# Neighbours' rows of places 640 to 960: a one-hot matmul gather replaced by indirect DMAs from lists made on the chip

## The chip, the cores and the metric

The kernel runs on one core of a Trainium2 chip. The metric is device time in microseconds (us). The core has a matrix engine (PE), three engines for elementwise work (DVE for vectors, ACT for activations and copies, POOL for everything irregular) and a queue engine (SP). Each takes its instructions in order; they wait for one another by semaphores. DMAs are issued from the queues of SP, ACT and POOL.

## The reference

Sixteen graphs of 1024 nodes with 64 channels. Layer 0 aggregates neighbours by quantiles, layer 1 is a three-step graph convolution. Both are preceded by a layer norm with relu and added to their input. Cut to what matters here:

```python
h = jnp.maximum(_layernorm(x, axis=-1), 0.0)
# layer 0: drop some neighbours of nodes with more than 10, keep each node itself
rem = neigh & (sk > 1) & (rank % sk == sk - 1) & mask[:, :, None]
rem = rem | jnp.swapaxes(rem, 1, 2)
nd = jnp.where(rem, 0.0, adj_) > 0
s = jnp.sort(jnp.where(nd[..., None], h[:, None, :, :], jnp.inf), axis=2)
nv = nd.sum(2)
for tau, w in ((0.25, 0.25), (0.5, 0.5), (0.75, 0.25)):
    pos = tau * (nv - 1)               # linear interpolation between the two nearest ranks
    agg += w * (v_lo + frac * (v_hi - v_lo))
x = x + (relu((h + agg) @ W1 + b1) @ W2 + b2) * mask
# layer 1: h = relu(layernorm(x)); three times relu(adj @ (h @ W) + b) with a batch norm
x = x + relu(concat(x1, x2, x3) @ Wl + bl)
```

So every node needs, channel by channel, the values of its 9 to 42 live neighbours in sorted order around three ranks. That sort is most of the work.

## The kernel before, in words

**Pairs and places.** Graphs are taken two at a time (a pair, eight in all): partitions 0 to 63 hold the channels of the first graph, 64 to 127 those of the second. `prepare` (L589) and `prepare_one` (L666) load the adjacency, work out which edges stay, count the live neighbours and give each node a place by that count (L786). The rows of the live matrix are scattered to their places in DRAM by eight indirect DMAs for each graph on POOL (L793, `live_d`) and loaded again in order (L807, `lp`). `find_live` (L819) turns them on PE (L827), sums chunks, and `number_slots` (L855) numbers each node's neighbours 1, 2, 3 and on: `st.r` holds, for every possible neighbour and node, the number of the slot or something else.

**Blocks.** Places are cut into seven blocks (L39) and a tail (L44), each with a number of slots as large as its largest count: 200 nodes with 11 slots, 192 with 13, 200 with 15, 176 with 17, 120 with 19, 72 with 21, 48 with 26, and 16 with 42.

**Gather.** `gather` (L976) fills g[channel, slot, node] by a matmul with a one-hot operand. For a group of slots DVE compares the numbers with the slot (L1004, tile `s`, two buffers), PE multiplies the features, split into three bfloat16 parts `st.hp`, with it (L1035), and ACT copies the sum from PSUM (L1040).

```python
nc.vector.tensor_scalar(
    s[:, k, :, us, w0:], r[:, :, us, at + w0 : at + W], float(LIVE + 1 + k0 + k), None, ALU.is_equal
)
```

**Sort.** `quantiles` (L942) runs a fixed network of min and max on DVE (L952) over g and a spare tile t. Missing neighbours are half zeros and half large numbers (`missing_high`), so the wanted ranks lie around the middle. ACT makes the interpolation weights (L885, L888), DVE multiplies them with the few rows that can be met (L958) and sums (L967). The result has channels on partitions; `store` (L1055) turns it on PE and ACT sends it to `agg_d`.

**Order.** The order is written by hand. `weave` (L1133) runs the sort of one block and, at given shares of it, steps of other generators: the gather of the next block, and `SHARES` (L31) steps of preparing the next pair. An iteration of the loop over pairs (L1468) sorts blocks 0 to 5 and then the 48 columns (`sort_pairs`, tile `agg_pairs`) beside the next pair's first gather. The 16-column tails of four pairs are sorted together in the fifth pair and in the last. A scheduler then puts each engine's instructions in the order in which it expects them to be ready. The last pair's sorts (L1501 on, called the late stage here) run beside `later` (L1255), the second part: for each pair `first` (L1261) fetches the aggregates back by node with 16 indirect DMAs on POOL (L1274, 128 rows of 256 bytes each), adds h (L1169) and does the first layer; `second` and `next_layer` (L1192) do the convolutions (L1227, L1232, L1250). It advances 7 steps (`STEPS`) with each sort, 56 in all; the other 72 of its 128 steps follow alone (called the tail of the run here).

## Time and profile before

Three runs took 3077.79, 3082.75 and 3086.61 us. The profiled execution's own time is its span, 3081.7 us; nothing outside the span is recorded for it.

| | us | share of the span | instructions |
|---|---|---|---|
| PE, matmuls | 2579.4 | 84% | 27857 |
| DVE | 2529.1 | 82% | 5606 |
| ACT | 1702.7 | 55% | 3284 |
| POOL | 473.6 | 15% | 425 |
| mean granted PE clock | 0.925 | | |

Busy time is the union of an engine's instructions. A group of instructions is given by line, engine, operation and tiles, with its count, busy time, mean duration in ns, and the idle time of the engine just before it with what ended that. An instruction on DVE starts some 78 ns before the one ahead of it ends, so durations add up to more than busy time. The time of a DMA instruction on POOL is that of the instruction alone; when its transfer lands is recorded apart (2.5 us after its issue for L1274 and 2.6 for L793, medians).

### The profile page before, as it was taken

Reading aid. Unit: us, or ns where it says so; the run is one execution under the profiler, and the core shown is the slowest. Engines: PE = TensorE matmul, PEld = TensorE weight load, DVE = VectorE, ACT = ScalarE, POOL = GpSimd, SP = SyncE. Lnnn points to the kernel's source line nnn. Section 1 sums busy time; section 2 is a strip of 40 time slices with the busy share of each in tenths; the row PEclk is TensorE's granted clock in tenths of the full one; section 3 lists DMA queues with packets and bytes.
Section 4 is the critical chain, followed back from the end, with each engine's and each line's share of the span. In section 5 each row is a group of like instructions: output and inputs, shape, how many; then the busy total and the mean of one; then the engine's idle time right before and its main releaser. Section 6 shows DMA issues by size and latency. Waiting matters only on the chain. (4 is left out here: it accounts for less than half of the span.)

```text
span 3081.7 us, 66749 instructions
## 1 busy us (share of the span) xinstructions
PE 2579.4 (84%) x27857; PEld 1706.2 (55%) x27857; DVE 2529.1 (82%) x5606; ACT 1702.7 (55%) x3284; POOL 473.6 (15%) x425
## 2 busy tenths in 40 slices
PE   2679998989898899885888989898886789887788
PEld 1446655665566556643665566566543456554456
DVE  4049999999999999999999999999986878963332
ACT  4774676568557756774478557756753222332222
POOL 5110130031003100500031004100503120121210
PEclk9789999999999899997998999899986889999989
DMA  4131022112111211232112211211222010122211
GB/s 142 42 116 57 17 66 69 64 45 71 62 64 45 80 60 44 65 81 22 56 66 61 72 50 56 80 51 44 72 34 58 12 50 11 50 57 55 58 53 43
DMA packets 219799, 177.43 MB, mean 58 GB/s; under 512 B 187744, under 2 KB 187872, under 8 KB 215392
## 3 DMA queue, kind: packets, MB, share of 16 engines
q1 hardware_dynamic: 141824, 125.88, 13.4%
q0 software_dynamic: 15872, 37.80, 4.0%
q10 hardware_dynamic: 61792, 9.39, 2.0%
q8 instruction: 220, 3.60, 0.5%
q14 instruction: 91, 0.75, 0.1%
HBM read 124.44 MB, written 48.55 MB: 56 GB/s over the span
## 5 line engine op out<-in xcount | busy, mean ns | idle before, releaser
L1035 PE MATMUL pg<-s,hp 128*64 128x400 bf16 (+11 forms) x16848 | 1385.7, 315 | 150.5 <-DVE s L1004 132.4
L1035 PEld LDWEIGHTS <-hp 128*64 128x64 bf16 x16848 | 903.9, 113 | 532.2 <-issue 116.0
L1004 DVE TENSOR_SCALAR s<-r 128x3200 bf16<-128x3200 bf16 (+25 forms) x1312 | 624.8, 524 | 53.9 <-PE pg L1035 51.8
L793 POOL DMA_INDIRECT live_d<-edge,place x128 | 271.9, 2124 | 1831.3 <-DVE place L786 1744.0
L1040 ACT COPY g<-pg 128x400 f32<-128x400 f32 (+6 forms) x350 | 153.2, 442 | 380.4 <-PE pg L1035 368.1
L1227 PE MATMUL pg<-adjT,xw 128*64 128x512 fp8e4 x2304 | 281.9, 398 | 56.4 <-DVE xw L1217 30.6
L952 DVE TENSOR_TENSOR t<-g 128x800 f32<-128x800 f32 (+20 forms) x416 | 295.5, 733 | 2.9 <-ACT g L1040 1.9
L952 DVE TENSOR_TENSOR g<-t 128x800 f32<-128x800 f32 (+5 forms) x392 | 264.7, 703 | 0.9
L1227 PEld LDWEIGHTS <-xw 128*64 128x64 bf16 x2304 | 147.6, 115 | 174.4 <-DVE xw L1217 32.3
L1274 POOL DMA_INDIRECT agg<-agg_d,place x128 | 133.8, 1045 | 588.7 <-PE pt L1158 128.2
L683 ACT ACTIVATE edge<-a 128x1024 fp8e4<-128x1024 f32 x128 | 134.7, 1055 | 144.8 <-DMA a<-in_adj 144.6
L885 ACT ACTIVATE coef<-z,bias 128x200 f32<-128x200 bf16 (+4 forms) x392 | 150.2, 423 | 100.7 <-DVE agg L967 65.9
L888 ACT ACTIVATE coef<-coef,wcol 128x200 f32<-128x200 f32 (+6 forms) x496 | 183.6, 405 | 6.2 <-issue 3.9
L685 DVE SCALAR_TENSOR_TENSOR junk_v<-a 128x1024 fp8e4<-128x1024 f32 x128 | 155.5, 1215 | 23.2 <-DMA a<-in_adj 23.2
L952 DVE TENSOR_TENSOR t<-t 128x600 f32<-128x600 f32 (+18 forms) x272 | 169.7, 632 | 0.4
L783 ACT ACTIVATE stays<-keys,minus 128x1024 fp8e4<-128x1024 f32 x128 | 143.2, 1119 | 38.1 <-PE keys L775 35.9
L764 ACT ACTIVATE edge<-q,bias 128x1024 fp8e4<-128x1024 f32 x128 | 141.8, 1108 | 31.3 <-PE q L759 31.3
L737 ACT ACTIVATE stays<-cs,back 128x1024 f16<-128x1024 f32 x128 | 136.1, 1112 | 34.0 <-DVE look L718 18.1
L868 ACT CAST r<-pr 128x592 bf16<-128x592 f32 (+1 forms) x256 | 141.2, 585 | 19.1 <-PE pr L864 11.8
L1231 ACT ACTIVATE xT<-pg,c_L_gnn_b 128x512 f32<-128x512 f32 x48 | 32.9, 685 | 208.7 <-PE pg L1227 208.6
L830 ACT ACTIVATE liveT<-pt 128x1024 fp8e4<-128x1024 f32 x128 | 126.5, 1028 | 26.4 <-PE pt L827 21.5
L690 PE MATMUL ptE<-ident_h,edge 128*128 128x128 bf16 x1024 | 85.7, 233 | 61.7 <-ACT edge L683 45.4
(186 smaller groups left out, 3889.0 us busy)
## 6 DMA issues: line engine op xcount, KB each, us to landing
a<-in_adj SPq DMA_DIRECT2D x128, 512.0 KB, 3.5
adjT_d<-edgeT SPq DMA_DIRECT2D x16, 1024.0 KB
lp<-live_d POOLq DMA_DIRECT2D x32, 512.0 KB, 5.3
adjT<-adjT_d SPq DMA_DIRECT2D x16, 1024.0 KB, 7.0
room<-in_x SPq DMA_DIRECT2D x16, 256.0 KB, 3.6
h_d<-room SPq DMA_DIRECT2D x16, 256.0 KB
h_again<-h_d SPq DMA_DIRECT2D x16, 256.0 KB, 4.6
old_hp<-h_d SPq DMA_DIRECT2D x16, 256.0 KB, 3.6
```

The lines of the kernel that those rows point to most:

```text
L685: nc.vector.scalar_tensor_tensor(junk, a, 1.0, a, ALU.is_equal, ALU.not_equal, accum_out=odd[:, b, t : t + 1], saturate=False)
L764: nc.scalar.activation(edge[:, t, :], q, AF.Relu, bias=bias(-2.0), accum_out=nv[:, t : t + 1], saturate=False)
L783: nc.scalar.activation(junk, keys, AF.Sign, bias=minus[:, t : t + 1], accum_out=above[:, t : t + 1], saturate=False)
L793: sent = nc.gpsimd.indirect_dma_start(out=live_d[b][:, :], out_offset=bass.IndirectOffsetOnAxis(ap=place[:, b, t : t + 1], axis=0), in_=ed ...
L868: nc.scalar.copy(st.r[side][:, x, u, :], pr[:, : j1 - j0])
L885: nc.scalar.activation(coef[:, i, :], z[:, at], AF.Abs, bias=bias(rank - (slots + 1) // 2 + tau), scale=sign)
L888: nc.scalar.activation(coef[:, i, :], coef[:, i, :], AF.Relu, bias=wcol[:, q : q + 1], scale=-w)
L952: nc.vector.tensor_tensor(view(bufs, o, n1, n2), view(bufs, a, n1, n2), view(bufs, b, n1, n2), ALU.max if op else ALU.min)
L1004: nc.vector.tensor_scalar(s[:, k, :, us, w0:], r[:, :, us, at + w0 : at + W], float(LIVE + 1 + k0 + k), None, ALU.is_equal)
L1035: summed = nc.tensor.matmul(out=pg[x * C : (x + 1) * C, ks, w0:], lhsT=st.hp[:, part, x, u, :], rhs=s[:, ks, x, u, w0:], start=(whole and ...
L1040: nc.scalar.copy(g[:, k0 : k0 + n, :], pg)
L1227: nc.tensor.matmul(out=pg[cs, :], lhsT=part[:, u, cs], rhs=adjT[x][:, u, sl], start=(u == 0 and k == 0), stop=(u == NT - 1 and k == len(xw ...
```

## The change

Places 640 to 960 leave the gather by matmul. The third block grows from 200 to 248 nodes (392 to 640), the three blocks behind it become `NODES`: places 640 to 768 with 17 slots, 768 to 896 with 19, 896 to 960 with 21. Only places below 640 and from 960 are numbered and held in `st.r`, `st.nvs` and `st.z`.

For the new ranges, PE makes for each node a row of 256 numbers (tile `pk`): each holds a group of four possible neighbours with a bit for each one that is live, and the group's index below. `list_rows` takes the 24 largest of them, eight at a time, with DVE's max and match_replace, splits them into single neighbours by the bits, takes the 24 largest again, and fills the rest with the numbers of a row of zeros or of large numbers. The result, `st.listed`, is a list of row numbers in `rows_d`, a DRAM copy of h in that order which SP writes by eight more DMAs for each pair.

`fetch_nodes` then issues, slot by slot, an indirect DMA on POOL of 128 rows of 256 bytes from `rows_d` to `g_nodes`, in which nodes lie on partitions: 34 DMAs for the first range (two graphs beside one another), 38 for the second, 42 for the third (two pairs beside one another, 64 nodes of each graph). `sort_nodes` sorts them with the same networks at a width of 128; the weights are one number for each node and are broadcast over channels, and the result goes to `agg_d` from SP without a turn.

`NODE_ORDER` gives the order of the twenty fetches. In an iteration of the loop the first node sort follows block 0, the second follows block 2; each fetch is issued when the node sort before it has been issued. The remaining six node sorts lie in the late stage, where `later` advances 98 steps. The tile g has the tags g0, g1 and gn with one buffer each instead of g with two, and `st.hp` one buffer instead of two.

```diff
-SHARES = (10, 9, 17, 24, 20, 13, 0)
-STEPS = 7
+SHARES = (18, 20, 13, 29, 17)
+LATE_SHARES = (8, 8, 8, 8, 8, 8, 10, 10, 10, 10, 10)
...
-BLOCKS = ((0, 200, 1, 11), (200, 392, 10, 13), (392, 592, 12, 15), (592, 768, 14, 17),
-          (768, 888, 16, 19), (888, 960, 17, 21), (960, 1008, 19, 26))
+BLOCKS = ((0, 200, 1, 11), (200, 392, 10, 13), (392, 640, 12, 15), (960, 1008, 19, 26))
+
+NODES = ((640, 768, 14, 17), (768, 896, 16, 19), (896, 960, 17, 21))
+
+NODE_ORDER = (
+    ((0,), 0), ((0,), 1), ((1,), 0), ((1,), 1), ((0, 1), 2), ((2,), 0), ((2,), 1), ((3,), 0), ((3,), 1), ((2, 3), 2),
+    ((4,), 0), ((4,), 1), ((5,), 0), ((5,), 1), ((4, 5), 2), ((6,), 0), ((6,), 1), ((6, 7), 2), ((7,), 0), ((7,), 1),
+)
...
+LISTED = 24
+MEMBER = 512
+ABOVE = 8192.0
+ZERO_ROW, BIG_ROW = 0, 1
+ROWS = 2 + 1024
...
-SPLIT = 592
+SPLIT = 640
+REST = 960
...
+    rows_d = [dram.tile([2 * ROWS, C], F32, name=f"rows_d{p}") for p in range(NP)]
...
+            for t in range(4):
+                row0 = x * ROWS + 2 + 256 * t
+                nc.sync.dma_start(
+                    out=rows_d[p][row0 : row0 + 256, :].rearrange("(u j) c -> j u c", j=32),
+                    in_=h[32 * t : 32 * t + 32, x],
+                )
...
+        listed = work.tile([P, 2 * len(NODES) - 1, 256], F32, tag="stays", name="listed")
+        st.nodes_nv = keep.tile([P, 2 * len(NODES) - 1], F32, tag="nodes_nv", bufs=2, name="nodes_nv")
...
-        st.z = keep.tile([P, len(TAUS), N], BF16, tag="z", name="z")
-        half = work.tile([P, N], F32, tag="a", bufs=2, name="half")
+            find_live[x] = yield from find_live[x](rows[x], listed)
+        yield from list_rows(st, listed, pools)
+        for x in range(2):
+            find_live[x]()
...
-        st.hp = keep.tile([P, 3, 2, NT, C], BF16, tag="hp", bufs=2, name="hp")
+        st.hp = keep.tile([P, 3, 2, NT, C], BF16, tag="hp", name="hp")
...
+    def list_rows(st, listed, pools):
+
+        work, keep, ps = pools
+        tiles = listed.shape[1]
+        top = work.tile([P, tiles, LISTED], F32, tag="a", bufs=2, name="top")
+
+        def largest(out, values):
+            for k in range(0, LISTED, 8):
+                nc.vector.max(out[:, k : k + 8], values)
+                if k + 8 < LISTED:
+                    nc.vector.match_replace(values, out[:, k : k + 8], values, -1.0e6)
+
+        for i in range(tiles):
+            largest(top[:, i], listed[:, i])
+            yield
+        single = work.tile([P, tiles, LISTED, 4], F32, tag="a", bufs=2, name="single")
+        nc.vector.tensor_tensor(
+            single.rearrange("p i k t -> p (i k) t").bitcast(I32),
+            top.rearrange("p i k -> p (i k)").bitcast(I32)[:, :, None].to_broadcast([P, tiles * LISTED, 4]),
+            member_bits.bitcast(I32)[:, None, :].to_broadcast([P, tiles * LISTED, 4]),
+            ALU.bitwise_and,
+        )
+        nc.vector.tensor_tensor(
+            single, single, base[:, :, None, :].to_broadcast([P, tiles, LISTED, 4]), ALU.add
+        )
+        for i in range(tiles):
+            largest(top[:, i], single[:, i].rearrange("p k t -> p (k t)"))
+        st.listed = keep.tile([P, tiles, LISTED], I32, tag="listed", bufs=4, name="rows_listed")
+        nc.vector.tensor_tensor(st.listed, top, fill, ALU.max)
+        yield
...
-            def number_slots(side):
-
-                j0, j1 = ((0, SPLIT), (SPLIT, N))[side]
+            pk = ps.tile([P, 4, 256], F32, tag="big", bufs=2, name="pk")
+            for i, (j0, _, _, _) in enumerate(NODES):
+                j0 -= x * C * (i == 2)
+                places = slice(j0, j0 + P)
+                nc.tensor.matmul(out=pk[:, i, :], lhsT=ones, rhs=groups_of, start=True, stop=False)
                 for u in range(NT):
-                    pr = ps.tile([P, N], F32, tag="big", bufs=2, name="pr")
-                    for a in range(j0, j1, HALF):
-                        sl, o = slice(a, min(a + HALF, j1)), slice(a - j0, min(a + HALF, j1) - j0)
-                        nc.tensor.matmul(out=pr[:, o], lhsT=upto, rhs=liveT[:, u, sl], start=True, stop=(u == 0))
-                        if u:
-                            nc.tensor.matmul(
-                                out=pr[:, o], lhsT=before[:, u : u + 1].to_broadcast([P, P]), rhs=sums[:, sl],
-                                start=False, stop=True,
-                            )
-                    nc.scalar.copy(st.r[side][:, x, u, :], pr[:, : j1 - j0])
-                    if u % 2:
-                        yield
-
-            return number_slots
+                    nc.tensor.matmul(
+                        out=pk[:, i, 32 * u : 32 * u + 32], lhsT=liveT[:, u, places], rhs=members,
+                        start=False, stop=(u == NT - 1),
+                    )
+                nc.tensor.matmul(
+                    out=pk[:, 3, i : i + 1], lhsT=sums[:, places], rhs=all_rows[:, :1], start=True, stop=True
+                )
+            nc.scalar.copy(listed[:, 2 * x : 2 * x + 2, :], pk[:, :2, :])
+            nc.scalar.copy(listed[half, 4, :], pk[half, 2, :])
+            nc.scalar.copy(st.nodes_nv[:, 2 * x : 2 * x + 2], pk[:, 3, :2])
+            nc.scalar.copy(st.nodes_nv[half, 4:5], pk[half, 3, 2:3])
+            yield
...
+            for u in range(NT):
+                pr = ps.tile([P, N], F32, tag="big", bufs=2, name="pr")
+                for a in range(0, SPLIT, HALF):
+                    o = slice(a, min(a + HALF, SPLIT))
+                    nc.tensor.matmul(out=pr[:, o], lhsT=upto, rhs=liveT[:, u, o], start=True, stop=(u == 0))
...
+                nc.scalar.copy(st.r[0][:, x, u, :], pr[:, :SPLIT])
+                if u % 2:
+                    yield
+            def number_rest():
+
+                pr = ps.tile([P, NT, N - REST], F32, tag="big", bufs=2, name="pr_rest")
...
+                nc.scalar.copy(st.r[1][:, x], pr)
...
-    def quantiles(pool, block, bufs, z, dst):
+    def quantiles(pool, block, bufs, z, dst, G=None):
...
+        coef = coefficients(pool, z, W if G is None else G, slots, order, "coef" if G is None else "node_coef")
+        prod = coef if G is None else pool.tile([P, len(order), W], F32, tag="coef", bufs=1, name="prod")
...
+            if G is None:
+                o, a, b = prod[:, i : i + n, :], view(bufs, spec, 1, n), coef[:, i : i + n, :]
+            else:
+                o = prod[:, i : i + n, :].rearrange("p n (g c) -> p n g c", c=C)
+                a = view(bufs, spec, 1, n, C)
+                b = coef[:, i : i + n, :, None].to_broadcast([P, n, G, C])
+            nc.vector.tensor_tensor(o, a, b, ALU.mult)
...
-        pool, tag, bufs = home or (rows, "g", 2)
+        pool, tag, bufs = home or (rows, f"g{n % 2}", 1)
...
+    def fetch_nodes(pairs, i, pools, tag):
+
+        work, ps, rows = pools
+        j0, j1, _, slots = NODES[i]
+        G = len(pairs) if i == 2 else 2
+        g = rows.tile([P, slots, G * C], F32, tag=tag, bufs=1, name="g_nodes")
+        for k in range(slots):
+            for a in range(G):
+                st = pairs[a if i == 2 else 0]
+                at = 4 if i == 2 else 2 * a + i
+                nc.gpsimd.indirect_dma_start(
+                    out=g[:, k, a * C : (a + 1) * C],
+                    out_offset=None,
+                    in_=rows_d[st.p][:, :],
+                    in_offset=bass.IndirectOffsetOnAxis(ap=st.listed[:, at, k : k + 1], axis=0),
+                )
...
+        return pairs, i, g, z
...
+    def sort_nodes(fetched, pools):
+
+        work, ps, rows = pools
+        pairs, i, g, z = fetched
+        j0, j1, _, slots = block = NODES[i]
+        W = g.shape[2]
+        t = rows.tile([P, plan(block)[3], W], F32, tag="t", bufs=1, name="t_nodes")
+        agg = work.tile([P, W], F32, tag="agg_nodes", bufs=1, name="agg_nodes")
+        yield from quantiles(work, block, (g, t), z, agg, W // C)
...
+            if i < 2:
+                nc.sync.dma_start(out=agg_d[2 * pairs[0].p + a][j0:j1, :], in_=agg[:, cols])
+            else:
+                for x in range(2):
+                    nc.sync.dma_start(
+                        out=agg_d[2 * pairs[a].p + x][j0:j1, :], in_=agg[x * C : (x + 1) * C, cols]
+                    )
...
+            sts = [ahead.result]
+            jobs = iter(NODE_ORDER)
+
+            def fetch_next(tag="gn"):
+                pairs, i = next(jobs)
+                return fetch_nodes([sts[p] for p in pairs], i, pools, tag)
...
+            nodes = fetch_next()
...
+                st = sts[p]
+                ahead = Steps(prepare(p + 1, early))
...
+                weave(sort_block(st, 0, pools), gather_block(st, 1, pools), steps(0))
+                weave(sort_nodes(nodes, pools), gather_block(st, 2, pools), steps(1))
+                nodes = fetch_next()
+                weave(sort_block(st, 1, pools), steps(2))
+                both = rows_of_pairs(MID, p, p + 1, p, pools, "g1")
+                weave(
+                    sort_block(st, 2, pools), gather_block(st, MID, pools, into=both),
+                    gather_block(st, MID + 1, pools, (early[0], "a", 2)), steps(3),
+                )
+                if p in TAILS:
+                    tails = rows_of_pairs(MID + 1, *TAILS[p], TAILS[p][1], pools, "g0")
+                weave(sort_nodes(nodes, pools), steps(4))
+                ahead.rest()
+                sts.append(ahead.result)
+                nodes = fetch_next()
+                if p in TAILS:
+                    weave(sort_pairs(MID + 1, *TAILS[p], tails, pools))
+                    send(pools)
+                weave(sort_pairs(MID, p, p + 1, both, pools), gather_block(sts[-1], 0, pools))
...
-            done.sent = TAILS[NP - 1][0]
+            done.sent = 4
...
-            for n in range(MID):
...
+            def steps(n):
+                return ahead, LATE_SHARES[n], 0.0, 1.0
...
+            st = sts[-1]
+            weave(sort_block(st, 0, pools), gather_block(st, 1, pools), steps(0))
+            weave(sort_nodes(nodes, pools), gather_block(st, 2, pools), steps(1))
+            nodes = fetch_next()
+            weave(sort_block(st, 1, pools), steps(2))
+            both = rows_of_pairs(MID, NP - 1, NP, NP - 1, pools, "g1")
+            weave(sort_block(st, 2, pools), gather_block(st, MID, pools, into=both), steps(3))
+            tails = rows_of_pairs(MID + 1, *TAILS[NP - 1], NP - 1, pools, "g0")
+            weave(sort_nodes(nodes, pools), gather_block(st, MID + 1, pools, into=tails[:, :, -TW:]), steps(4))
+            nodes = fetch_next()
+            weave(sort_pairs(MID + 1, *TAILS[NP - 1], tails, pools), steps(5))
+            send(pools)
+            done.sent = NP - 2
+            more = fetch_next("g0")
+            weave(sort_nodes(nodes, pools), steps(6))
+            nodes = fetch_next()
+            weave(sort_pairs(MID, NP - 1, NP, both, pools), steps(7))
+            send(pools)
+            weave(sort_nodes(more, pools), steps(8))
+            done.sent = NP - 1
+            more = fetch_next("g0")
+            weave(sort_nodes(nodes, pools), steps(9))
+            weave(sort_nodes(more, pools), steps(10))
             send(pools)
             done.sent = NP
             ahead.rest()

```

## The prediction

> **What bounds the kernel now.** I read first the busy times of each engine stretch by stretch, cut at the ends of the 48-column sorts (one per pair of graphs). Columns: stretch, length, then PE, PEld, DVE, ACT, POOL busy with counts, granted clock, DMA share, GB/s.
>
> ```profile
> 517.30:806.90 289.60, 260.51 (x3043) 172.21 (x3041) 278.80 (x607) 193.51 (x374) 43.72 (x20) 0.95 0.20 62
> 806.90:1097.50 290.60, 261.01 (x3043) 172.06 (x3041) 277.44 (x605) 192.88 (x373) 37.95 (x20) 0.95 0.20 61
> ...
> 2297.20:2748.30 451.10, 351.17 (x3287) 237.90 (x3287) 357.26 (x813) 134.47 (x330) 87.76 (x80) 0.86 0.18 41
> 2748.30:3081.70 333.40, 275.62 (x2145) 178.06 (x2144) 110.48 (x157) 80.45 (x131) 45.99 (x48) 0.92 0.19 52
> ```
>
> An ordinary iteration of the loop takes 290 us and VectorE (DVE) is busy for 279 of them: the loop is bound by DVE, with PE at 90% beside it and POOL nearly idle. The late stage (451 us, last pair's sorts beside the first 56 steps of the second part) has both at 78%; the tail (333 us, the other 72 steps) is a PE chain. Six loop iterations, one with a tail sort, take 1780 us from 517.3 to 2297.2. Then the groups, for prices:
>
> ```profile
> L1035 PE MATMUL pg<-s,hp 128*64 128x400 bf16 (+11 forms) x16848 | 1385.7, 315 | 150.5 <-DVE s L1004 132.4
> ...
> L1004 DVE TENSOR_SCALAR s<-r 128x3200 bf16<-128x3200 bf16 (+25 forms) x1312 | 624.8, 524 | 53.9 <-PE pg L1035 51.8
> L793 POOL DMA_INDIRECT live_d<-edge,place x128 | 271.9, 2124 | 1831.3 <-DVE place L786 1744.0
> ...
> L1274 POOL DMA_INDIRECT agg<-agg_d,place x128 | 133.8, 1045 | 588.7 <-PE pt L1158 128.2
> ```
>
> L1004 and L1035 are the gather that three of eight blocks lose. L1274 is the same operation as each new gather (128 rows of 256 B by an index column), so the kernel before prices it. The timeline of POOL shows how that price moves:
>
> ```profile
> 659.50 20.19 POOL L793 DMA_INDIRECT live_d<-edge,place  x1 [212.03 <-DVE place L786]
> 679.99 1.35 POOL L793 DMA_INDIRECT live_d<-edge,place  x1 [0.30 <-issue]
> 681.64 1.16 POOL L793 DMA_INDIRECT live_d<-edge,place  x1 [0.30 <-issue]
> ```
>
> ```profile
> 2466.28 1.79 POOL L1274 DMA_INDIRECT agg<-agg_d,place  x1 [67.47 <-DVE s L1004]
> 2468.37 1.86 POOL L1274 DMA_INDIRECT agg<-agg_d,place  x1 [0.30 <-issue]
> ...
> 2481.17 0.94 POOL L1274 DMA_INDIRECT agg<-agg_d,place  x1 [0.31 <-issue]
> ```
>
> Alone it is 0.94 + 0.30 = 1.25 us per gather. Beside a dense DVE it is 1.3 to 1.9 us busy. Once in each of the seven loop iterations, the first indirect DMA took 13.5 to 20.2 us (mean 17.4, sum 122); the other 121 of L793 average (271.9 - 122) / 121 = 1.24, so 1.54 with the 0.30.
>
> **What the Trainium skill says.** "SBUF — State Buffer", section "SBUF: two separate sides", says that GpSimd writes the descriptors of its DMAs through ports shared with DVE, and that DVE's two-port operations lock it out. The trace agrees in kind: the seven long waits end about 0.9 us after a DVE gap or an operation reading PSUM. In the other direction I see nothing: 704-wide TENSOR_TENSORs take 884 ns without an indirect DMA beside them and 882 with one. "VectorE: DVE Perf Modes", section "The TRN2 errata", gives a fixed term and one element a cycle for fp32 tensor_tensor, (N+151)/0.96 ns; the trace has 884 at N=704 (formula 891). The section "Two Vector instructions with no wait between them" of the same page says that MATCH_REPLACE_8 goes with a MATCH_VALUE_LOAD, two instructions; no run here shows it.
>
> **Part 1, removed gather work.** I counted elements in the built instruction list. Comparisons fall from 1312 to 856 instructions and from 1.858 to 1.181 million columns, 0.64 on either count: 624.8 x 0.36 = 225 us of DVE, 28 per pair. Slots times nodes fall from 16400 to 10336 per pair: PE loses 0.37 x 1385.7 / 8 = 64 us per pair. The wide slot numbering, evictions and masks of these blocks go too (about 9 PE, 15 ACT per pair, estimated by the same shares). ACT has 96 us idle per iteration, so its part is worth nothing.
>
> **Part 2, sorts.** Elements are nearly the same (1.019 to 1.007 million), instructions fall from 2958 to 2730. At 72 ns + 1.04 ns per element (from 980 ns at 800, 250 at 96, less 78 of overlap) that is 1272 to 1244 us: 3.5 per pair. Shorter z rows: 1.5. A node sort costs 26.5 us of DVE on average (20 of them, 530). A pair owns two and a half, but the loop does two per iteration and the late stage six: 13 us per iteration move to the late stage, where 3.5 x 26.5 = 93 arrive.
>
> **Part 3, the lists.** Per pair 30 max instructions and 20 match_replace, half on 256 columns, half on 96, and two operations on 480. At the tensor_tensor price with 100 ns for the second instruction: 7.7 + 7.1 + 1.1, with small ones 17 us. No row shows them. Bounds: 6 us (fixed terms alone) and 32 us (two passes); I take 17. PE gets 60 small matmuls, about 8 us, in its slack.
>
> DVE per iteration: 279 - 28 - 3.5 - 1.5 + 17 - 13 = 250. Summing the list between the ends of the 48-column sorts gives 248, 256, 248, 305 (tails), 251, 239: 1547 for the six. PE gets to about 195, so DVE bounds more clearly. Idle DVE is (1780 - 1709) / 6 = 12 us an iteration now; I keep 13. Loop: 1547 + 78 = 1625.
>
> **Part 4, POOL.** The gathers are 17 x 2 + 19 x 2 + 21 = 93 per pair, 744 in all; 78 per iteration. Pitch: not below 1.25, not above about 18.8 (every one a long wait). I take 1.6, between the 1.54 above and 2466-2480's 1.85. An iteration: 78 x 1.6 + 16 x 1.6 (live_d) + 5 = 155 of 263 us, hidden. Cover of each fetch: the first is issued when the second node sort ends and needed after the 48-column sort and block 0's sort, 90 us later, against 60; the second has block 1's and 2's sorts, 76 us, against 60 plus the first graph's live_d, 13. Just covered. Uncovered it costs the excess in DVE time. In the built POOL order live_d stands inside the second fetch and lp behind it; queued behind lp are the second graph's live_d and lp, and PE's in-order transposes (pt), with the gathers, wait for those. New waits: a node sort's first DVE operation waits for its last gather (2.5 us to land, as L1274 shows), and behind it in DVE's order stand the comparisons of the next channel block, so PE as well; the loop's cover above is what hides it. hp has one buffer instead of two, so ACT's cast into it waits for the pair's last gather; that ends with the third sort, a 30 us node sort earlier: zero, and if it came late the next pair's first gather would start late by as much. The new 64 KB row writes on SP (8 per pair) and the node results' stores are needed tens of us later: zero.
>
> **Part 5, start and end.** The first pair's lists are exposed, some +5, the first iteration is 24 shorter: first mark at 498. Late stage: steps done there rise from 56 to 98 of 128. DVE: 357 - 25 (comparisons) + 93 + 42 x 110.5 / 72 (64) = 489. PE: 351 - 63 + 42 x 275.6 / 72 (161) = 449. POOL: 186 gathers and some 100 of L1274, 286 x 1.6 = 458. Three engines in order, all close: at 83% of the busiest, 590 us (bounds 500 and 660). Tail: 30 steps at 333.4 / 72 = 4.6, less a little for the last pair without a successor: 125.
>
> Sum: 498 + 1625 + 590 + 125 = 2838; I say **2835**. The profiled span, 3081.7, stands 1 us under the median of the runs, so no correction.
>
> **Rivals.**
> - **The port** (slower). DVE's back-to-back sorts hold POOL out. If one gather in ten meets the 17.4 us wait, pitch is 1.6 + 1.6 to 1.7 = 3.3: an iteration becomes 78 x 3.3 + 31 = 288, the late stage 186 x 3.3 + 154 = 768; 505 + 1728 + 768 + 125 = **3126**. It decides from a mean pitch near 3.2. For it: seven waits in 128. Against: the other 121, and L1274 in dense sorts.
> - **The queue.** Lists come late behind fetches, PE stalls on pt and DVE with it: 25 us more in seven iterations = **3010**. For it: the just-covered second fetch. Against: PE's 60 us of slack.
> - **Dense.** The node sorts need no PE, so the late stage runs at 500 and idle falls to 8 per iteration: 498 + 1595 + 505 + 120 = **2718**.
> - **Not as said.** A list overflow turns on the general path, milliseconds. Against: the counts are tested as before, with nearly the same bounds.
>
> **Numbers.** Likeliest 0.52 (2835), queue 0.17, dense 0.12, port 0.15, general path 0.01, and 0.03 for gains lost to within 0.3%, about what a measurement here can tell from no change. Faster 0.81, same 0.03, slower 0.16. The range, 2715 to 3040, takes in dense, queue and a list price at its upper bound (+15 x 8 = 120); the port and half of the low end stay out.
>
> **What would show it.** Iterations near 263 with DVE at 250; comparisons at 400 us; max and match_replace together near 118; the new gather at 1.2 to 1.6 us mean without long waits; late stage near 590, 30 steps of tail. Wrong if gathers average over 2.9 us, if DVE waits for g_nodes by more than some us per sort, or if pt waits for lp.

## The result, and the profile after

The kernel after takes 3092.2 us (median of 6 runs, 3084.6 to 3109.2), the kernel before, on the same chip, 3078.5 (6 runs, 3075.2 to 3086.6). The ratio is 1.0045, 95% interval 1.0023 to 1.0067: the same to within 0.7%, and if anything a little slower. The forecast was 2835, faster. The profiled execution of the kernel after has a span of 3089.0 us.

First the stretches of the kernel after, cut as before at the ends of the 48-column sorts, with two more cuts at the last node sort and the end. Columns as in the prediction.

```profile
528.70:801.70 273.00, 208.95 (x2453) 146.00 (x2455) 248.13 (x566) 173.11 (x336) 148.26 (x107) 0.84 0.26 78
...
1951.70:2249.80 298.10, 195.96 (x2361) 140.34 (x2359) 238.77 (x557) 163.93 (x323) 146.00 (x117) 0.83 0.25 71
2249.80:2749.10 499.30, 329.04 (x3051) 226.51 (x3048) 366.28 (x789) 131.17 (x330) 266.60 (x207) 0.82 0.22 42
2749.10:2946.40 197.30, 117.53 (x886) 74.20 (x882) 122.47 (x238) 40.36 (x89) 81.56 (x76) 0.81 0.21 51
2946.40:3089.00 142.60, 117.44 (x955) 77.31 (x955) 42.93 (x61) 31.12 (x50) 15.41 (x16) 0.92 0.16 50
```

The first of these iterations has DVE busy for 248 us, as forecast (248), but takes 273 and not 261. Now the groups that answer to those of before, and the new ones:

```profile
L1283 POOL DMA_INDIRECT g_nodes<-rows_d,rows_listed x744 | 1027.3, 1381 | 1089.0 <-DVE prod L1093 486.5 <-DVE t_nodes L1081 242.0 <-issue 213.7
...
L1143 DVE TENSOR_SCALAR s<-r 128x3200 bf16<-128x3200 bf16 (+19 forms) x856 | 407.7, 521 | 137.8 <-PE pg L1174 130.1 <-ACT r L982 7.5
...
L890 POOL DMA_INDIRECT live_d<-edge,place x128 | 161.1, 1258 | 235.9 <-DVE place L883 174.1 <-DVE s L1143 25.5 <-issue 21.6
...
L710 DVE MAX8 top<-listed 128x8 f32<-128x256 f32 x120 | 45.2, 415 | 53.4 <-ACT listed L966 53.4
...
L712 DVE MATCH_REPLACE8 listed<-top,listed 128x256 f32<-128x256 f32 x80 | 32.2, 408 | 0.0
...
L712 DVE MATCH_VALUE_LOAD listed<-top,listed 128x8 f32 x80 | 6.3, 78 | 0.0
```

The comparisons cost 407.7 us (400 forecast). The gather by list costs 1.38 us and 0.30 to the next, 1.68 (1.6 forecast). Max and match_replace, with their 96-column forms of 24.1 and 18.7 us, add up to 120.2; together with a short load ahead of each match_replace, and with overlaps counted once, they keep DVE busy for 115.9 (118 forecast). The work is where and as large as the sum had it. The waits are not:

```profile
DVE agg L1351 <- DMA agg<-agg_d,place: 233.3, 8, 53.4
...
DVE s L1143 <- PE pg L1174: 130.1, 21, 21.8
PE pt L924 <- DMA lp<-live_d: 105.9, 7, 21.4
PE pg L1174 <- ACT hp L695: 93.2, 6, 17.1
```

(Columns: us in total, times, longest.) In the kernel before, the second was 51.8 (the prediction's line for L1004), the third is not among its waits, the fourth was 8.7, and the first was:

```profile
DVE agg L1169 <- DMA agg<-agg_d,place: 84.6, 8, 13.9
```

DVE's busy time fell from 2529.1 to 2411.2 us, by 118; its idle time rose from 552.6 to 677.8, by 125. What the change saved in work, it gave back in waits. By stage, idle DVE went from 165 to 193 up to the first mark, from 71 to 177 in the six iterations, and from 317 to 308 in the late stage and tail, where the forecast had some 180.

Why PE stands at `pt` (the transposes of the ordered live rows `lp`), POOL's timeline of one iteration shows (the columns are start, duration, line, operation, and in brackets the idle time ahead of it and what ended that):

```profile
908.83 1.06 POOL L1283 DMA_INDIRECT g_nodes<-rows_d,rows_listed  x1 [0.31 <-issue]
910.20 1.73 POOL L890 DMA_INDIRECT live_d<-edge,place  x1 [0.30 <-DVE t L1081]
...
922.30 0.96 POOL L890 DMA_INDIRECT live_d<-edge,place  x1 [0.30 <-issue]
923.57 1.38 POOL L1283 DMA_INDIRECT g_nodes<-rows_d,rows_listed  x1 [0.31 <-issue]
...
966.26 0.94 POOL L1283 DMA_INDIRECT g_nodes<-rows_d,rows_listed  x1 [0.30 <-issue]
967.20 1.62 POOL L904 DMA_DIRECT2D lp<-live_d  x2
```

The places of the graph are known at 900.2. Nine gathers of the second fetch go first, then the eight scatters, then the fetch's remaining gathers, and only behind them the load `lp`. By an estimate from the issue of the last scatter at 922.30 and the 2.6 us from issue to landing in the kernel before, it was ready at about 925. PE's first `pt` starts at 971.5. From place to `pt` it is 62 to 74 us in the seven loop iterations; in the kernel before, 45 to 47.

The aggregates of the second part stand behind a fetch in the same way, in the late stage and once before it: the sixteen gathers for the first pair, at 2224 in the last iteration of the loop, follow a fetch that ran from 2157, and DVE stands at their sum for 39.3 us there. One case of the late stage:

```profile
2866.87 0.94 POOL L1283 DMA_INDIRECT g_nodes<-rows_d,rows_listed  x1 [0.30 <-issue]
2868.12 0.94 POOL L1454 DMA_INDIRECT agg<-agg_d,place  x1 [0.31 <-issue]
...
2886.83 0.95 POOL L1454 DMA_INDIRECT agg<-agg_d,place  x1 [0.30 <-DMA agg<-agg_d,place]
```

The fetch ran from 2812 to 2868, the sixteen gathers of aggregates after it, and DVE stood in order at the sum with h, with the rest of a node sort behind it:

```profile
2889.57 1.23 DVE L1351 TENSOR_TENSOR agg<-agg,h_late 128x1024 f32<-128x1024 f32 x1 [46.29 <-DMA agg<-agg_d,place]
```

### The profile page after: what moved, and what is told of

The parts are those of the page before. It is cut to its first block, busy times and chain, and to the rows that moved or that the text cites. A ratio compares the mean times of both kernels' runs of the same rounds, so it can differ in the third digit from the quotient of the medians.

```text
span 3089.0 us, 58573 instructions
## 1 busy us (share of the span) xinstructions
PE 2131.9 (69%) x23401; PEld 1472.7 (48%) x23401; DVE 2411.2 (78%) x5602; ACT 1558.7 (50%) x3060; POOL 1385.5 (45%) x1155
## 5 line engine op out<-in xcount | busy, mean ns | idle before, releaser
L1283 POOL DMA_INDIRECT g_nodes<-rows_d,rows_listed x744 | 1027.3, 1381 | 1089.0 <-DVE prod L1093 486.5
L1174 PE MATMUL pg<-s,hp 128*64 128x248 bf16 (+6 forms) x12048 | 890.5, 302 | 250.4 <-DVE s L1143 132.3
L1174 PEld LDWEIGHTS <-hp 128*64 128x64 bf16 x12048 | 643.7, 114 | 434.4 <-issue 128.7
L1143 DVE TENSOR_SCALAR s<-r 128x3200 bf16<-128x3200 bf16 (+19 forms) x856 | 407.7, 521 | 137.8 <-PE pg L1174 130.1
L890 POOL DMA_INDIRECT live_d<-edge,place x128 | 161.1, 1258 | 235.9 <-DVE place L883 174.1
L924 PE MATMUL pt<-ident_h,lp 128*128 128x128 bf16 x1024 | 94.1, 249 | 153.4 <-DMA lp<-live_d 105.9
L1179 ACT COPY g<-pg 128x248 f32<-128x248 f32 (+3 forms) x238 | 98.0, 413 | 190.2 <-PE pg L1174 182.7
L1351 DVE TENSOR_TENSOR agg<-agg,h_late 128x1024 f32<-128x1024 f32 x8 | 9.8, 1225 | 233.3 <-DMA agg<-agg_d,place 233.3
L1081 DVE TENSOR_TENSOR t<-g 128x800 f32<-128x800 f32 (+9 forms) x184 | 166.3, 922 | 3.8 <-ACT g L1179 3.2
L1081 DVE TENSOR_TENSOR g<-t 128x992 f32<-128x992 f32 (+7 forms) x176 | 159.8, 932 | 1.8
L1010 ACT ACTIVATE coef<-z,bias 128x200 f32<-128x200 bf16 (+2 forms) x208 | 89.3, 480 | 116.9 <-DVE agg_pairs L1102 67.2
L787 PEld LDWEIGHTS <-edge 128*128 128x128 fp8e4 x1024 | 67.5, 106 | 143.4 <-ACT edge L780 102.5
```

The lines of the kernel that those rows point to most:

```text
L787: nc.tensor.matmul(out=pt[:, u, :], lhsT=edge[:, t, u * P : (u + 1) * P], rhs=ident_h, start=True, stop=True)
L890: sent = nc.gpsimd.indirect_dma_start(out=live_d[b][:, :], out_offset=bass.IndirectOffsetOnAxis(ap=place[:, b, t : t + 1], axis=0), in_=ed ...
L924: nc.tensor.matmul(out=pt[:, u, :], lhsT=lp[:, u * P : (u + 1) * P], rhs=ident_h, start=True, stop=True)
L1081: nc.vector.tensor_tensor(view(bufs, o, n1, n2), view(bufs, a, n1, n2), view(bufs, b, n1, n2), ALU.max if op else ALU.min)
L1143: nc.vector.tensor_scalar(s[:, k, :, us, w0:], r[:, :, us, at + w0 : at + W], float(LIVE + 1 + k0 + k), None, ALU.is_equal)
L1174: summed = nc.tensor.matmul(out=pg[x * C : (x + 1) * C, ks, w0:], lhsT=st.hp[:, part, x, u, :], rhs=s[:, ks, x, u, w0:], start=(whole and ...
```

## The experiments

My theory after the result: the work is as forecast, and what it freed went into waits in order behind the list gathers on POOL, some in the loop (`lp`), some in the late stage (`agg`), with a part lost at the start. The rivals: PE's wait for the single feature buffer; DVE or PE themselves slowed (ports, clock); a late stage that is a chain of the second part and would take its time anyway. Nine kernels were run.

**e1: two buffers for the features.** For even pairs hp lies in the pool of `prepare`.

```diff
-        st.hp = keep.tile([P, 3, 2, NT, C], BF16, tag="hp", name="hp")
+        st.hp = (keep if p % 2 else work).tile([P, 3, 2, NT, C], BF16, tag="hp", name="hp")
```

To make room, two small tiles became 16 bits wide and the two small result tiles of the sorts share a buffer.

> The pair's split features (hp) get a second buffer again, for even pairs in the preparing pool, so that ACT's cast no longer waits for the last gather of the pair before; nothing else moves (the order of PE's, ACT's and POOL's instructions is the same). Theory (new waits in order ate the gain): PE's 93 us of waiting for hp (six times, up to 17.1) go, and since DVE stands behind PE then, the loop gets 40 to 80 us shorter: 3010 to 3050 us. Rival (the slack hides it, as the prediction said): PE waits for something else instead, within 10 us of 3092.

Measured: 3100.1 us, ratio to before 1.0051 (1.0028 to 1.0075), no difference from 1.0045. And the wait is still there, as long as it was:

```profile
PE pg L1174 <- ACT hp L695: 94.4, 6, 17.1
```

So it was never the buffer. The waits name the one that writes, not what held it up. ACT's cast waits 0.2 us for its input; it is SP that waits before it, 94.5 us in eight times in the kernel after, to load h:

```profile
SPq L693 <- DVE rows_listed L730: 94.5, 8, 22.3
```

The load of h takes a buffer that the lists use (tag a), and DVE ends these late. What this wait is worth was not tried; e5 bounds it for the kernel in which `lp` does not wait.

**e2: `lp` on SP's queue.** One word of `fetch` in `prepare_one`:

```diff
-                load = nc.gpsimd.dma_start(
+                load = nc.sync.dma_start(
```

> The ordered live rows (lp) are loaded from SP's queue instead of POOL's, so that they no longer stand behind a fetch of list rows; the scatters (live_d) stay where they were. Theory (queueing on POOL): PE's 106 us of waiting for lp shrink to under 40 us and the loop gets 20 to 60 us shorter: 3030 to 3070. Rival: the scatters themselves stand inside the fetch and set the time, so the wait stays at 80 or more and the run at 3080 to 3095.

Measured: 3177.4 us, ratio 1.0320 (1.0303 to 1.0338), 85 us slower than the kernel after. Neither theory had this. The wait at `pt` for `lp` is gone from the list, and in its place there are:

```profile
PE tot L755 <- DVE edgeT L795: 258.8, 14, 42.9
DVE edgeT L795 <- DMA adjT_d<-edgeT: 206.8, 11, 43.9
```

(60.7 and 6.8 in the kernel after.) On SP the load waits in order for the scatters (SP stands there for 737 us in all), and the next graph's store of `adjT_d` waits behind it; DVE may not change `edgeT` before that store, PE not go on before DVE. The load left one queue and blocked another: from place to `pt` it is now 69 to 92 us.

**e3: the constant rows sent early.** The tile `filler` lay in a pool that took over the memory of the set-up before it, so its first write waited 12.6 us for the set-up's DMAs, and ACT, which issued its sixteen DMAs in order, 16.2 us with the first graph's casts behind it.

```diff
     with tc.tile_pool(name="setup", bufs=2) as setup:
+        filler = setup.tile([2, C], F32, name="filler")
...
-                nc.scalar.dma_start(out=rows_d[p][x * ROWS + ZERO_ROW : x * ROWS + BIG_ROW + 1, :], in_=filler)
+                nc.gpsimd.dma_start(out=rows_d[p][x * ROWS + ZERO_ROW : x * ROWS + BIG_ROW + 1, :], in_=filler)
```

> The two constant rows of each rows_d are made and sent ahead of the bounds, from POOL's queue, instead of after them from ACT's; ACT then has no wait of 16.2 us for them at the start. Theory: the first 48-column sort ends 14 to 18 us earlier (528.7 to about 512) and the whole run is 12 to 18 us shorter: 3074 to 3080. Rival: the wait comes back as one for adjacency or scatters, and the run stays within 5 us of 3092.

Measured: the first mark (the end of the first 48-column sort) at 516.1 instead of 528.7, 12.6 earlier. Of the whole run 6.6 us arrive: 3085.6, ratio 1.0015 (1.0001 to 1.0030), whose interval overlaps that of the kernel after. Both gains fall short of the theory's, 14 to 18 and 12 to 18. Shown for the start, not settled for the end.

**e4: the aggregates used later.** In `later`, the next pair's gathers go out after the first step of a pair, their first use comes after the seventh.

```diff
+            taken = 0
             while now.step():
                 yield
-                if ahead is not None and ahead.step():
+                taken += 1
+                if ahead is not None and (taken == 1 or taken > 6) and ahead.step():
                     yield
```

> In the second part, the 16 gathers of a pair's aggregates are issued in its predecessor's first step and used only after its seventh, instead of right behind; same work, same number of steps. Theory (in the late stage the aggregates queue on POOL behind fetches of list rows and DVE stands in order behind them): DVE's 233 us of waiting at the sum with h fall below 100, the late stage and the tail together get 80 to 140 us shorter: 2950 to 3010. Rival (the late stage is a chain of PE and POOL work that takes its time anyway): the wait turns up in front of another instruction and the run stays within 20 us of 3092.

Measured: 3030.5, ratio 0.9847 (0.9827 to 0.9866), 62 us less than the kernel after: the theory's direction, less than its 80 to 140. The wait at the sum with h fell from 233.3 to 146.5, not below 100. The stretches of e4 (late stage, tail) show that nearly all of the gain lies in the late stage (696.6 in the kernel after) and the tail (142.6):

```profile
2247.80:2890.40 642.60, 456.46 (x4016) 306.36 (x4013) 486.99 (x1024) 172.17 (x418) 348.44 (x282) 0.85 0.22 48
2890.40:3021.70 131.30, 109.13 (x872) 69.26 (x871) 45.24 (x64) 30.81 (x50) 15.48 (x16) 0.93 0.20 58
```

**e5: `lp` ahead of the rest of the fetch.** The second fetch is written after block 1, and from its seventeenth gather on it is told to stand behind the next pair's first loads. In the two traces DVE's and SP's instructions come in the same order, PE's and ACT's too but for a few neighbours that change places; POOL's order differs.

```diff
-                nodes = fetch_next()
                 weave(sort_block(st, 1, pools), steps(2))
+                nodes = fetch_next(behind=2 * p + 2)
...
+                if behind is not None and k * G + a >= 16:
+                    tc.add_manual_dep(
+                        got.ins, loads[behind].ins.name,
+                        mybir.DependencyInfo(mybir.DependencyClass.NoSync, mybir.DependencyReason.SCHED_ONLY),
...
```

> The second fetch of each iteration is cut in two: its first 16 gathers go as before, the rest stand on POOL behind the next pair's first scatters and loads (live_d and lp of its first graph). The order on PE, DVE and ACT is the same, and no work is added or taken. Theory (lp stands behind the fetch, PE stands at pt, and DVE in the loop waits for PE's gather): place to pt of the first graph falls from 62-74 us to some 40-50, PE's 106 us of waiting for lp fall below 40, DVE's waiting for pg (95 us in the loop) below 50, and the run gets 40 to 100 us shorter: 2990 to 3050. Rival (PE's slack takes it up, as with the feature buffer): within 10 us of 3092; or the second node sort comes to wait for its gathers, then slower.

Measured: 2988.6, ratio 0.9712 (0.9696 to 0.9728): 104 us less than the kernel after, and faster than before, without an instruction more or less. The waits:

```profile
DVE s L1144 <- PE pg L1175: 17.4, 14, 6.3
...
PE pt L925 <- DMA lp<-live_d: 1.6, 1, 1.6
```

and the stretches (the first iteration, the last one, the late stage):

```profile
508.50:767.50 259.00, 207.59 (x2453) 146.82 (x2457) 248.02 (x566) 173.44 (x336) 153.48 (x108) 0.86 0.27 82
...
1855.90:2143.10 287.20, 194.41 (x2357) 139.15 (x2356) 238.49 (x556) 164.37 (x323) 148.56 (x117) 0.84 0.26 73
2143.10:2844.30 701.20, 449.92 (x3932) 298.76 (x3928) 488.84 (x1026) 171.61 (x418) 353.42 (x282) 0.81 0.21 44
```

The first five iterations stand 11.0, 6.7, 4.3, 10.3 and 8.9 us above DVE's busy time, the last one 48.7, of which 38.9 are the wait at the sum with h. From place to `pt` it is 47 to 54 us. The wait for hp is unchanged (94.8) and PE's slack takes most of it: in the first five iterations it can cost no more than those 4 to 11 us. The six iterations sum to 1634.6 us; the forecast said 1625. The late stage has not got shorter.

**e6: no gathers by list.** One plain DMA for each graph, of fixed rows, in place of 34 to 42 gathers; the kernel leaves out the selection, and the bytes stay the same:

```diff
-        for k in range(slots):
-            for a in range(G):
...
-                nc.gpsimd.indirect_dma_start(
-                    out=g[:, k, a * C : (a + 1) * C],
+        for a in range(G):
...
+            nc.gpsimd.dma_start(
+                out=g[:, :, a * C : (a + 1) * C],
...
```

> Leaves out the selection: each fetch brings fixed rows with one plain DMA for each graph (same bytes, same buffer and order) instead of 34 to 42 gathers by list, so POOL hardly issues anything; lists are still made. Theory (what was lost is waiting behind the gathers in POOL's order): lp and the aggregates no longer queue, the loop gets 60 to 110 us shorter, the late stage and the tail 90 to 160: 2830 to 2940. Rival (what was lost is PE's and ACT's own pace and the chain of the second part, or DVE slowed by the lists): 3000 or more.

Measured: 2831.8, ratio 0.9192 (0.9175 to 0.9209), a hair above the lower end of what the theory gave. The six iterations are 123 us shorter than in the kernel after, more than its 60 to 110. An iteration, the late stage and the tail:

```profile
510.40:763.20 252.80, 201.49 (x2447) 143.81 (x2451) 247.10 (x566) 173.20 (x336) 29.72 (x24) 0.89 0.27 83
...
2108.40:2690.10 581.70, 444.68 (x3931) 298.33 (x3927) 488.02 (x1026) 171.48 (x418) 141.50 (x106) 0.88 0.24 54
2690.10:2832.80 142.70, 117.41 (x957) 76.79 (x955) 42.94 (x61) 31.11 (x50) 15.55 (x16) 0.93 0.16 50
```

POOL is busy for 30 us of an iteration instead of 148, and DVE's work is 247.1 instead of 248.1: the gathers cost DVE's own work nothing by being issued beside it. In the kernel after, DVE also waited for the gathered rows themselves for 6.9 us only. So nearly all of the 260 us that the gathers cost is idle time, and the waits that shrink without them are the three of POOL's other work: `pt` for `lp`, the comparisons behind it (18.1 us instead of 130.1) and the sum with h (93.2 instead of 233.3). That no other effect of the gathers has a part in it is not shown. Nor is 2831.8 a floor for other orders: in e8 below, the start and the tail are shorter than here.

**e7: e3, e4 and e5 together.**

> Three edits together: constant rows sent early, aggregates used later, second fetch behind the next pair's scatters. Theory: the gains add, 10 at the start, 40 to 100 in the loop, 60 in the late stage: 2930 to 2990, faster than the kernel before by 3 to 5%. Rival (they share one wait): no better than the best alone, 3030.

Measured: 2925.6, ratio 0.9499 (0.9481 to 0.9517). The single gains, 7 + 62 + 104 = 173, add up to within a few us of the 167 measured, as three separate waits would. The theory's range, 2930 to 2990, was a little too high.

**e8: e7, and two buffers for the aggregates of the second part.** A remainder kept in SBUF before goes to PSUM for room.

```diff
-            agg = one.tile([P, NT, 2, C], F32, tag="agg", name="agg")
+            agg = one.tile([P, NT, 2, C], F32, tag="agg", bufs=2, name="agg")
...
-                    rest = one.tile([P, 4, XC], F32, tag="rest", name="rest")
+                    rest = pw
```

> The three edits together, and in the second part two buffers for the aggregates, so that their gathers need not wait on POOL for the transposes of the pair before, with a fetch of list rows queued behind them; to make room, a remainder is kept in PSUM. Theory (in the late stage POOL stands in waits, 57 and 66 us at two gathers of aggregates, and blocks what is queued behind): DVE's 143 us of waiting at the sum with h and its 41 for list rows together fall below 120, the run to 2870 to 2910. Rival (the late stage is held by the chain of the second part on PE): within 10 us of 2926.

Measured: 2884.0, ratio 0.9366 (0.9350 to 0.9382), 42 us less than e7 and well under both kernels that are compared. The late stage and the tail:

```profile
2137.60:2760.40 622.80, 450.59 (x4018) 309.67 (x4015) 485.72 (x1023) 171.02 (x418) 349.21 (x278) 0.85 0.22 49
2760.40:2884.80 124.40, 105.93 (x870) 68.84 (x869) 44.46 (x64) 30.45 (x50) 15.64 (x16) 0.94 0.21 61
```

The time fits the theory, its figure for the waits does not: DVE still waits at the sum with h for 143.6 us in total, now in four long ones instead of seven (142.9), and for list rows for some 24 (41). What fell is the time for which POOL itself stood blocked at a gather of aggregates: 184.8 us, all for the transposes of the pair before, in e7; 39.6 for them and 59.6 for a later reader in e8. The edit changes two things at once (the buffer, and where the remainder lies), so its share is not shown to be the buffer's alone. And of the 43.6 us between the two profiled executions only 28 lie in the late stage and the tail, where nearly all of the second part runs (646.0 and 129.6 in e7); why the start and the loop are 15 shorter is not shown.

**e9: no lists, on top of e7.**

```diff
-            largest(top[:, i], listed[:, i])
...
-        nc.vector.tensor_tensor(st.listed, top, fill, ALU.max)
+        nc.vector.tensor_copy(st.listed, fill)
```

> Leaves out the lists on top of the three edits: no max, no match_replace, no splitting; every list is the constant filling (all gathers read a zero row or a large one), all else is issued as before. DVE loses some 17 us for each pair. Theory (with the queue mended the loop is bound by DVE again): each loop iteration gets 13 to 17 us shorter, the start 15, the run 95 to 125 shorter than the three edits: 2800 to 2830. Rival (PE or the queues bound the loop, DVE's lists lie in idle time): under 50 us shorter, 2880 or more.

Every list is then the constant filling. Measured: 2863.0 (2848.4 to 2867.9), ratio 0.9307 (0.9292 to 0.9323), 63 us less than e7, between the two. Two ordinary iterations and, between them, the one with a tail sort:

```profile
480.30:723.00 242.70, 204.64 (x2482) 143.89 (x2484) 232.78 (x491) 172.88 (x333) 120.20 (x91) 0.91 0.43 84
...
1221.50:1561.40 339.90, 211.75 (x2498) 149.88 (x2496) 293.04 (x701) 183.02 (x375) 177.79 (x110) 0.80 0.42 66
1561.40:1802.90 241.50, 200.59 (x2486) 142.04 (x2486) 232.67 (x493) 172.94 (x336) 113.25 (x83) 0.93 0.47 83
```

In e7 these took 261.5, 318.2 and 259.4. They and a third ordinary one (240.4, in e7 256.1) lose 15 to 18 us of DVE and 16 to 19 us of time: there the loop is bound by DVE, us for us. The one with the tail sort got 22 us longer with 11 us less DVE, by a wait of the edit's own:

```profile
DVE rows_listed L715 <- DMA g_nodes<-rows_d,rows_listed: 37.6, 3, 33.4
```

The longest of the three lies in that iteration. The filling needs no input now and comes early in DVE's order; it writes one of four buffers, and stands until the gathers of two earlier pairs have read them. The transfers changed too: the DMA engines are busy for 0.42 to 0.48 of these stretches, for 0.26 to 0.29 in e7, at about the same GB/s. So the run as a whole is no price of the lists; the ordinary iterations are.

## Why the prediction was wrong

The forecast's four terms against the runs (us; each row adds up to its span but for rounding):

| | to the first mark | six iterations | late stage | tail | sum |
|---|---|---|---|---|---|
| forecast | 498 | 1625 | 590 | 125 | 2838 |
| kernel after | 528.7 | 1721.1 | 696.6 | 142.6 | 3089.0 |
| e5, `lp` ahead | 508.5 | 1634.6 | 701.2 | 142.3 | 2986.6 |
| e6, no gathers by list | 510.4 | 1598.0 | 581.7 | 142.7 | 2832.8 |
| e8: e3, e4, e5 and the second buffer | 497.6 | 1640.0 | 622.8 | 124.4 | 2884.8 |

*Parts 1 to 3* held. DVE in the six iterations: 1544 us against 1547. In the late stage: 488.7 against 489, PE 447 against 449. The rule drawn from them, that the loop is DVE's busy time plus some 13 us an iteration, failed in the kernel after (29 on average). In e5 the average is 15, but that is partly luck: five iterations have 4 to 11 and the last 49. In Part 3, match_replace does come with a second instruction, as the prediction assumed; it costs a step of 67 ns instead of the assumed 100.

*Part 4* is where it broke first. It had the price (1.6 against 1.68) and it had the facts: "In the built POOL order live_d stands inside the second fetch and lp behind it". But it called POOL's work "hidden" and the second fetch "Just covered", by testing the cover of the fetch: is the fetch done before its node sort? It was, with 23 us to spare at 967. The cover that failed is that of what stands behind the fetch, which the sum put at nothing. A load that in the kernel before had gone out as soon as its scatters were done waited for the rest of a 60 us fetch, PE stood at `pt`, and, PE being in order, the gather behind `pt` was late for DVE. The prediction's own sign of being wrong, "if pt waits for lp", is what the trace has: 105.9 us. The rival "queue" named this very chain and put it at 25 us an iteration with a chance of 0.17; "PE's 60 us of slack", the argument against it, is a mean over an iteration and says nothing about a wait that falls on one place in PE's order. Mending it alone gave 104 us, by the two profiles 86 in the six iterations and 20 before them, with a late stage 5 longer. The single buffer of hp was rightly put at zero (e1).

*Part 5* broke too, in the late stage: "Three engines in order, all close: at 83% of the busiest". The busiest, DVE, was busy for 70% of it. An engine's busy time in a stage does not tell for how long others wait for it, if it holds its work in order. POOL was busy for 348 of 697 us (with the 0.30 after each instruction about 433, near the 458 counted), and DVE stood for 181 of its 208 idle us at the sum with h. Without the fetches' gathers that wait is 71 and the stage 581.7 us, close to the 590. So it is the gathers that make it; how fetches and aggregates block one another on POOL, each waiting there for what DVE and PE release, is read from the traces and not tried apart. Using the aggregates later and giving them a second buffer, with the remainder in PSUM, brought the stage from about 700 to 622.8. The tail's 142.6 against 125 is no matter of the gathers (142.7 without them): 30 steps at 4.6 are 139, and what was taken off for the last pair did not come. With the aggregates used later it is 131, with the rest of e8 124.

The start: 31 us over the forecast. The 12.6 of the constant rows were overlooked: the prediction counted the new row writes, not the filler and its pool. Another 20 are the same queue, since the second pair is prepared before the first mark (e5: 508.5). With both mended the mark lies at 502.0 in e7 and 497.6 in e8, forecast 498.

The other rivals: the port is refuted as far as these runs go. The mean pitch was 1.68 us, far from the 3.3 that it needed: 14 of the 744 gathers took more than 5 us, none more than 11.6, where it had one in ten at 17.4. "Dense" did not happen, though e6 comes near it in the loop (1598.0 against 1595). A lower PE clock (0.845 against 0.925 granted) goes with PE's gaps: 0.95 where PE is busy for 90% of a stretch, 0.81 and 0.82 where it is for 60 to 66%. In e6 it is 0.876 without harm, so it is no cause that I could show.

That 2831.8 of e6 agrees with the 2835 forecast is partly luck (its loop is shorter, its start and tail longer), but it says what the forecast was: the time of this change if nothing had to stand behind the gathers. Of the 42 us in the loop by which e8 is still above e6, the last iteration (285.5 against 257.6) holds 28, and there DVE's wait at the sum with h explains it: 39.4 us against 12.7, for the first pair's aggregates, whose place behind a fetch no edit changed. In the late stage (41 us) that wait is 22 longer than in e6, DVE waits 13 for list rows, and the rest is spread. What a better order would win there stays open.

## What to carry to other kernels

When a burst of instructions is put on a quiet in-order queue, cost the work that already goes there, one item at a time: when was each ready, how much of the burst now stands ahead of it, who waits for it, and what stands behind that waiter; whether the burst itself is done in time answers another question. The wait it causes need not show on that queue: here it read as VectorE waiting for a matmul. Try the mend by order before one by another queue: here putting one load ahead of half a burst won 104 us, and moving it to another queue lost 85.

## What the runs showed of the hardware

- MAX8 over 256 fp32 columns took 415 ns and MATCH_REPLACE8 408 (242 and 238 over 96). That is near what the formula of "VectorE: DVE Perf Modes", section "The TRN2 errata", which the prediction cites for fp32 tensor_tensor, gives for one pass as an estimate: (256 + 151) / 0.96 = 424 ns. The Trainium skill says in "VectorE: DVE Perf Modes", section "Two Vector instructions with no wait between them", that MATCH_REPLACE_8 goes with a MATCH_VALUE_LOAD, and the trace agrees: each of the 160 has one ahead of it, of 64 to 92 ns, and starts 67 ns after it (median).
- The Trainium skill, "SBUF — State Buffer", section "SBUF: two separate sides", has GpSimd's descriptor writing share ports with VectorE. In the direction from POOL to DVE the runs show no cost: 248.1 us of DVE in an iteration with 148 us of POOL beside it, 247.1 with 30.
- The waits of 13.5 to 20.2 us at the first scatter of each iteration are gone: 2.7 us is the longest of the 128 scatters in the kernel after (161.1 us in all, from 271.9), and 2.6 in e6 (e5 and e8 have single ones of 5.7 and 7.9). In the kernel before, each of the seven came after 206 to 265 us in which POOL ran nothing, and the four other indirect DMAs after more than 60 us of idleness (67.5 to 122.9) took 1.0 to 1.8 us. In the kernel after POOL is never idle for more than 114.4 us ahead of an indirect DMA, in e6 for no more than 63.1. So the long scatters went with long idleness; whether that makes them, or the ports that the prediction put them down to, was not tried. The gathers by list have shorter waits without any: one at 937.25 took 8.2 us with 0.30 us of idle time ahead.
